# Last adds of a two-layer transformer stack written into the resident token rows, their transfers issued from two engines

## The chip, the cores and the metric

One core of a Trainium2 chip runs the whole kernel. The metric is the device time of one execution in microseconds (us). The kernel before was run five times: 1055.75, 1056.3, 1054.87, 1055.21 and 1051.39 us, with a median of 1055.21 us.

A core has five engines that run side by side, each with its own list of instructions: TensorE (PE, matmuls; its weight loads are shown apart as PEld), VectorE (DVE), ScalarE (ACT), GpSimd (POOL) and SyncE (SP). They wait for one another through semaphores. A transfer between the on-chip memory (SBUF) and the device memory (HBM) is issued by one of them, here mostly SP, and carried out by 16 DMA engines, which count a semaphore up, one step each, when their share has landed. Matmuls write into PSUM, a small memory of banks, from which DVE or ACT takes the results.

## The reference

The input is x, 2048 tokens of 256 numbers (f32). Four blocks are added to it one after the other, each reading the layer-normed tokens:

```python
x = x + _L0_xcond_ref(_layernorm(x), ctx, ctx, ...)    # 16-head attention over 1601 context rows
x = x + _L0_ffn_ref(_layernorm(x), ...)                # one of 8 experts for each token
x = x + _L1_xcond_ref(ctx, _layernorm(x), ...)         # attention in a window of the context
x = x + _L1_ffn_ref(_layernorm(x), ...)                # 64 slots
return x
```

The change lies in the end of the last one. There each token has weights `alpha` over 64 slots. The slots gather the tokens by these weights, go through a gated update and an attention among themselves, and give `slot_values`; then

```python
out = jnp.einsum('bts,bsd->btd', alpha, slot_values)
return out @ wo + bo
```

and the result is that plus x, 2048 x 256 numbers or 2 MB.

## The kernel before

The tokens live in SBUF from the first load to the end, in the tile `x_sb`, 128 partitions by 16 rows by 256 (token t*128 + p is row t of partition p). Every block adds its part to `x_sb` in place.

The first attention fills most of the span: for each block of 512 tokens and each group of four heads it searches the largest score of each token (L257, L262), computes scores and exponentials (L904, L909) and weighs the values (L870). Its order is written out by hand in Python as a list of steps that are put between the matmuls. Then come the experts (L1064, L1071), with the window attention and the slots' weights of earlier tokens as generators beside them: `aside` takes one step from each in turn. The program keeps the written order on each engine (`manual_schedule`), and the tile framework adds the semaphore waits. It knows which slice of a tile an instruction reads or writes.

The two generators leave behind, for each token block: `x_sb` with the window attention's part (L1258, POOL) and with the bias `bso` (L1335, POOL); the transposed weights `aT`, in which partitions 0 to 63 hold a rounded part and 64 to 127 the remainder (L1390, L1392); and the slots' sums in `psi`.

From L1439 on a single chain is left: the slots are updated, attend to one another, are normed (L1524) and are multiplied by the product of two weight matrices (L1527 to L1533). The result stands in PSUM as 128 x 256 and is split into two parts, by ACT (L1536) and DVE (L1537).

The last loop, L1541 to L1553, makes the output in eight turns of two token rows each (256 tokens). In each turn

- PE writes four matmuls into one PSUM bank (`f_ps`, L1546): for each of the two rows one with each part. `bank` hands out three banks in turn, so the matmuls of turn t wait until the add of turn t-3 has read its bank.
- DVE adds the bank to the rows of `x_sb`, one instruction of 128 x 512 (L1552), and writes the sum to a tile `o` of 2 KB in each partition. `o` comes from the pool `moe` with `bufs=3`, so there are three buffers, and the add of turn t waits until the transfer of turn t-3 has landed on all 16 DMA engines.
- SP issues the transfer of `o`, 256 KB, to the output (L1553), when the add is done.

Nothing else is left to do on ACT, POOL or the DMA engines in this loop. The program ends (L1629) when SP has seen the landing of all transfers, and the engines have met.

Of the kernel before, what the change touches and what calls it, by code (L numbers as in the profile page):

```python
# [10 lines left out]
F32 = mybir.dt.float32  # L11
# [4 lines left out]
ALU = mybir.AluOpType  # L16
# [3 lines left out]
P = 128  # L20
T = 2048
D = 256
# [40 lines left out]
def body(ctx: ExitStack, tc: tile.TileContext, a: dict, out: bass.AP):  # L63
    nc = tc.nc
# [5 lines left out]
    x_sb = keep.tile([P, NT, D], F32, name="x_sb")  # L70
# [109 lines left out]
    with (  # L180
# [49 lines left out]
        def two():  # L230
            return ps_s.tile([P, 2, LB], F32, tag="psc", name="s_ps")
# [508 lines left out]
        with (  # L740
# [137 lines left out]
            for u in range(NU):  # L878
                acc = None
                for i in range(NS):  # L880
# [16 lines left out]
                    for pl in range(2):  # L897
                        slot = (u * NS + i) * 2 + pl
                        look(slot)
                        ps = two()  # L900
# [35 lines left out]
    moe = ctx.enter_context(tc.tile_pool(name="moe", bufs=2))  # L936
# [7 lines left out]
    def bank(shape, name):  # L944
        n = int(np.prod(shape[1:]))
        ps = ps_pool.tile([P, LB], F32, tag="ps", name=name)[: shape[0], :n]
        if len(shape) == 3:
            ps = ps.rearrange("p (a b) -> p a b", a=shape[1])
        return ps
# [541 lines left out]
    for wt, b, name in ((wsq, bsq, "q4"), (wsk, bsk, "k4")):  # L1491
        ps = bank([NSLOT, NSLOT], name + "_ps")
# [10 lines left out]
    ps = bank([NSLOT, NSLOT], "qk_ps")  # L1503
# [11 lines left out]
    ps = bank([NSLOT, NSLOT], "pt_ps")  # L1515
# [3 lines left out]
    ps = bank([NSLOT, D], "sc_ps")  # L1519
# [8 lines left out]
    ps = bank([P, D], "s2_ps")  # L1528
# [11 lines left out]
    o_out = out.rearrange("(t p) d -> p t d", p=P)  # L1540
    for t2 in range(NT // 2):  # L1541
        ps = bank([P, 2, D], "f_ps")
        for k in range(2):
            t = t2 * 2 + k
            for w in range(2):
                nc.tensor.matmul(  # L1546
                    ps[:, k, :], aT[:, t * P : (t + 1) * P], parts[w],
                    start=w == 0, stop=w == 1,
                )
        o = moe.tile([P, 2, D], F32, name="o", bufs=3)  # L1550
        tl = slice(t2 * 2, t2 * 2 + 2)
        nc.vector.tensor_tensor(o, x_sb[:, tl, :], ps, ALU.add)  # L1552
        nc.sync.dma_start(o_out[:, tl, :], o)  # L1553


def lay_out(i):
# [76 lines left out]
```

## Time and profile before

| | us |
|---|---|
| median of the five runs | 1055.21 |
| the profiled execution | 1053.24 |
| its span | 1051.5 |
| span from the last split (L1536) to the end | 15.4 |
| DVE busy with the eight adds (L1552) | 5.2 |
| PE busy with the 32 matmuls of the loop (L1546) | 5.8 |
| idle time of DVE before an add, put down to transfers of `out_x` | 4.4 |

The span is the time from the first to the last instruction in the trace, and the profiled execution's own time is 1.7 us more. The profiled execution lies 2.0 us below the median. PE is busy for 90% of the whole span, DVE for 71%, ACT for 49%; in the last loop none of them is. A row of the page's groups gives an engine, a line, an operation, the tiles (output <- inputs), the shapes, the count, the busy time and the mean of one, and then how long the engine had been idle before, and for what. The chain of waits goes back from the last instruction, at each step to what released it.

### The profile page before, as it was taken

The page shows a single profiled execution, that of the slowest core. Times are in us where ns is not written, and L with a number is a line of the kernel's source. Part 1 is how long each engine was busy: PE and PEld are TensorE (multiplying, and loading weights), DVE is VectorE, ACT ScalarE, POOL GpSimd, SP SyncE. Part 2 cuts the span into 40 slices and gives each one's busy share as a digit, 9 for nine tenths or more (in the row PEclk, how much of TensorE's full clock was granted, in tenths as well). Part 3 has the DMA queues.
Part 4 walks back from the last instruction along what each step waited for, and adds up shares of the span by engine and source line. Part 5 has one row for each costly group of instructions (what it writes and reads, how often), then busy time and mean ns, then how long its engine had stood idle before and what let it go on. Part 6 is the DMA issues. An engine that isn't in the chain of part 4 may idle for free.

```text
span 1051.5 us, 14892 instructions
## 1 busy us (share of the span) xinstructions
PE 945.3 (90%) x5814; PEld 442.4 (42%) x5822; DVE 744.8 (71%) x1407; ACT 519.7 (49%) x614; POOL 71.8 (7%) x96
## 2 busy tenths in 40 slices
PE   7788888999988999998899999899979999989885
PEld 3244333444443344443343444343334464546543
DVE  7466868888877888877788887875054648585744
ACT  2423456676656666656666775667810012121430
POOL 4000200000010000000000000000030102111210
PEclk9998999999999999999999999989999999999998
DMA  5754721310102201101211011000080000000002
GB/s 173 162 148 101 145 74 46 110 29 2 29 2 82 65 2 29 29 1 39 82 29 29 2 29 29 1 2 1 2 230 1 1 0 1 1 1 0 1 1 81
DMA packets 32277, 46.98 MB, mean 45 GB/s; under 512 B 6411, under 2 KB 21268, under 8 KB 31950
## 3 DMA queue, kind: packets, MB, share of 16 engines
q1 hardware_dynamic: 30478, 43.65, 15.3%
q10 hardware_dynamic: 1232, 1.61, 0.4%
q8 instruction: 46, 0.75, 0.3%
q0 software_dynamic: 496, 0.76, 0.3%
q14 instruction: 25, 0.20, 0.1%
HBM read 26.77 MB, written 14.04 MB: 39 GB/s over the span
## 4 chain that ended last, share of the span: by engine, by line
PE 68%; DVE 25%; issue 4%; DMA 2%; ACT 1%; POOL 1%; POOLq 0%; SPq 0%; DVEq 0%; ACTq 0%
PE acc L870 18%; PE s_ps L904 14%; DVE mx L262 12%; PE a_ps L257 11%; PE y_ps L1064 7%; DVE xn L107 2%; DVE x_sb L1071 2%; PE a_ps L498 1%; PE o_ps L1250 1%; PE a_ps L845 1%; DVE ln_stats L96 1%; PE a_ps L240 1%; PE s_ps L627 1%; PE a_ps L284 1%; PE x_ps L461 1%
## 5 line engine op out<-in xcount | busy, mean ns | idle before, releaser
L262 DVE TENSOR_REDUCE mx<-a_ps 128x2 f32<-128x804 f32 (+1 forms) x637 | 490.8, 806 | 124.3 <-PE a_ps L257 117.7
L909 ACT ACTIVATE es<-s_ps 128x1024 f32<-128x1024 f32 (+1 forms) x416 | 408.3, 1022 | 201.9 <-PE s_ps L904 198.6
L257 PE MATMUL a_ps<-kb,qb 50*128 50x402 bf16 x992 | 218.1, 341 | 49.0 <-DVE mx L262 40.2
L904 PE MATMUL s_ps<-qt,kt 52*128 52x512 f32 (+1 forms) x832 | 236.7, 517 | 1.5 <-DMA qt<-nT 1.4
L870 PE MATMUL acc<-es,v 128*32 128x512 f32 (+1 forms) x1664 | 224.6, 611 | 0.0
L257 PEld LDWEIGHTS <-qb 50*128 50x128 bf16 x1024 | 77.5, 93 | 295.7 <-issue 281.9
L904 PE MATMUL s_ps<-ql,kt 52*128 52x512 f32 (+1 forms) x832 | 190.6, 394 | 0.0
L904 PEld LDWEIGHTS s_ps<-qt,kt 52*128 52x128 f32 (+1 forms) x832 | 97.1, 188 | 31.8 <-ACT es L909 16.7
L904 PEld LDWEIGHTS s_ps<-ql,kt 52*128 52x128 f32 (+1 forms) x832 | 103.0, 185 | 0.6
L1064 PE MATMUL y_ps<-expert_wT_sb,xT 128*128 128x512 f32 x192 | 89.8, 598 | 0.0
L102 POOL TENSOR_TENSOR ln_rstd<-ln_ve,mhalf 128x2 f32<-128x2 f32 (+2 forms) x28 | 21.1, 754 | 752.2 <-DVE ln_ve L100 750.9
L1071 DVE SCALAR_TENSOR_TENSOR x_sb<-y_ps,r_gate,x_sb 128x256 f32<-128x256 f32 x96 | 46.3, 482 | 32.5 <-PE y_ps L1064 30.7
L870 PEld LDWEIGHTS acc<-es,v 128*32 128x32 f32 (+1 forms) x1664 | 33.1, 108 | 42.3 <-issue 40.5
L1064 PEld LDWEIGHTS y_ps<-expert_wT_sb,xT 128*128 128x128 f32 x192 | 34.1, 191 | 31.9 <-issue 30.8
L1027 ACT COPY xT<-tr_ps 128x512 f32<-128x512 f32 (+1 forms) x28 | 13.4, 494 | 53.3 <-PE tr_ps L1024 53.3
L107 DVE TENSOR_SCALAR xn<-x_sb,ln_mv,ln_rstd 128x256 f32<-128x256 f32 x64 | 33.6, 568 | 1.1 <-POOL ln_rstd L102 1.1
L819 DVE RECIPROCAL rec<-a_ps 128x16 f32<-128x16 f32 x16 | 4.0, 253 | 42.7 <-PE a_ps L240 42.7
L1064 PE MATMUL y_ps<-expert_wT_sb,xnT 128*128 128x512 f32 x64 | 32.3, 632 | 0.0
L1024 PE MATMUL tr_ps<-ident,xn 128*128 128x128 f32 x88 | 17.6, 297 | 10.9 <-DVE xn L107 10.9
L96 DVE BATCH_NORM_STATS2 ln_stats<-x_sb 128x6 f32<-128x256 f32 x64 | 23.3, 413 | 3.4 <-POOL x_sb L1258 3.4
L1071 DVE SCALAR_TENSOR_TENSOR x_sb<-y_ps,gate,x_sb 128x256 f32<-128x256 f32 x32 | 15.5, 483 | 13.7 <-PE y_ps L1064 13.1
L997 PE MATMUL busy_ps<-xnT 128*128 128x512 bf16 x91 | 23.5, 387 | 0.4 <-issue 0.2
(347 smaller groups left out, 724.5 us busy)
## 6 DMA issues: line engine op xcount, KB each, us to landing
qt<-q_rows SPq DMA_DIRECT2D x32, 192.0 KB
q_rows<-qhi SPq DMA_DIRECT2D x8, 512.0 KB
qb<-q_rows SPq DMA_DIRECT2D x30, 96.0 KB
kt<-expert_wT_sb SPq DMA_DIRECT2D x24, 100.5 KB
q_rows<-qp SPq DMA_DIRECT2D x8, 256.0 KB
q_rows<-qlo SPq DMA_DIRECT2D x8, 256.0 KB
ql<-q_rows SPq DMA_DIRECT2D x32, 64.0 KB
expert_wT_sb<-in_expert_wT SPq DMA_DIRECT2D x1, 2048.0 KB
```

The lines of the kernel that those rows point to most:

```text
L96: nc.vector.bn_stats(stats[:rows, i, :], src[:, i, :])
L102: nc.gpsimd.tensor_tensor(rstd[:rows, :n], ve[:rows, :n], mhalf[:rows, :n], ALU.pow)
L107: nc.vector.tensor_scalar(dst[:, i, :], src[:, i, :], mv[:rows, i, 0:1], rstd[:rows, i : i + 1], ALU.subtract, ALU.mult,)
L257: nc.tensor.matmul(ps[:, k, :CH], qb[u % 2][rows, pl, t * P : (t + 1) * P], kb[g][rows, pl, c * CH : (c + 1) * CH], start=True, stop=True,)
L262: nc.vector.tensor_reduce(flat[:, n : self.n], ps[:, : self.n - n, :CH], AX.X, ALU.max)
L870: nc.tensor.matmul(acc[HP * j : HP * (j + 1), :], v[:n, i, h * VW : h * VW + HP], es[j // 2][:n, j % 2, :], start=i == 0, stop=i == NS - 1,)
L904: nc.tensor.matmul(ps[:n, h, :], kt[u % NG][rows, pl, i * P : i * P + n], q[u % nq][rows, pl, :], start=k == 0, stop=k == 1,)
L909: nc.scalar.activation(e[:n], ps[:n], AF.Exp)
L997: nc.tensor.matmul(calm[0].rearrange("p e d -> p (e d)"), xnT[:, 1, :P].bitcast(BF16)[:, 1::2], xnT[:, 0, :].bitcast(BF16)[:, 1::2], start ...
L1024: nc.tensor.transpose(ps[:, t * P : (t + 1) * P], xn[:, t, c * P : (c + 1) * P], ident)
L1064: nc.tensor.matmul(ps.rearrange("p e d -> p (e d)"), xT[:, c, tok], ew[:, c, pair * 2 * D : (pair + 1) * 2 * D], start=c == 0, stop=c == 1,)
L1071: nc.vector.scalar_tensor_tensor(xb[:, t, :], ps[:, k, :], gate[:, t, e : e + 1], xb[:, t, :], ALU.mult, ALU.add,)
```

## The change

The tile `o` is gone. The add writes its sum over the two token rows that it has read, in `x_sb`, and the transfer reads from there. The transfers of the even turns are issued by SP, as before, those of the odd turns by ACT.

```diff
-        o = moe.tile([P, 2, D], F32, name="o", bufs=3)
         tl = slice(t2 * 2, t2 * 2 + 2)
-        nc.vector.tensor_tensor(o, x_sb[:, tl, :], ps, ALU.add)
-        nc.sync.dma_start(o_out[:, tl, :], o)
+        nc.vector.tensor_tensor(x_sb[:, tl, :], x_sb[:, tl, :], ps, ALU.add)
+        (nc.scalar if t2 % 2 else nc.sync).dma_start(o_out[:, tl, :], x_sb[:, tl, :])
```

In the list of instructions with their waits, nothing else differs. The eight adds wait for PE alone, where five of the eight waited for a transfer as well. SP issues four transfers in place of eight, and ACT four after its last copy (L1536). The lines after the loop have moved up by one, so that the add is L1551, the transfer L1552 and the end of the program L1628.

## Prediction

> **What bounds the kernel now.** I read the end first, since the list of instructions differs only in the last loop. The busy time by stage gives the frame: from 1036 to 1051.5 us PE is busy 5.9 us of 15.5, DVE 5.6, ACT 0.4. No engine bounds this stage. The chain of waits, asked for its last part (start, duration, what), shows what does:
>
> ```profile
> 1037.66 0.70 DVE o L1552
> 1038.36 0.02 issue
> 1038.37 4.40 DMA out_x<-o
> ...
> 1042.89 0.70 DVE o L1552
> 1043.59 0.02 issue
> 1043.61 2.17 DMA out_x<-o
> ...
> 1045.90 0.70 DVE o L1552
> ...
> 1046.68 0.69 DVE o L1552
> ```
>
> Two landings, 4.40 and 2.17 us, stand between adds: the three buffers of `o` are full, and the fourth add waits for the first transfer, the seventh for the fourth. The views of the waits, first DVE's, then SP's (waiting line <- what for: total, times, longest), say the same and add the end of the program:
>
> ```profile
> DVE o L1552 <- DMA out_x<-o: 4.4, 2, 3.4
> ```
>
> ```profile
> SPq L1629 <- DMA out_x<-o: 2.3, 2, 1.7
> ```
>
> One landing takes 4.40 us and the other 2.17 for the same 256 KB. The view of the transfer's line gives the least, median and greatest time of one issue in ns, and the table of 1-us windows gives the engines' busy time, the granted clock, and last the DMA engines' mean share and rate:
>
> ```profile
> L1553 SPq DMA_DIRECT2D out_x<-o x8: 372/373/2092, 1038.4 to 1047.4; - x8
> ```
>
> ```profile
> 1040.00:1041.00 1.00, 0.34 (x3) 0.13 (x2) 0.00 (x0) 0.00 (x0) 0.00 (x0) 1.00 0.77 263
> 1041.00:1042.00 1.00, 0.00 (x0) 0.00 (x0) 0.00 (x0) 0.00 (x0) 0.00 (x0) 1.00 0.05 10
> 1042.00:1043.00 1.00, 0.00 (x0) 0.00 (x0) 0.11 (x1) 0.00 (x0) 0.00 (x0) 0.52 0.80 268
> ```
>
> From 1041 to 1042 the 16 DMA engines are nearly idle although a third transfer has been asked for. The trace's packet records say why. At 1039.53 one 16 KB packet of instructions (queue q8) starts and takes 1.74 us. The page counts 46 such packets, one for about every 128 PE instructions, so I take them for PE's code. It occupies one DMA engine: of the 16 steps of the first transfer's semaphore 15 come by 1040.56, the last at 1042.77; of the second, by 1041.28 and at 1043.41; of the third, by 1043.41 and at 1044.04. SP's third issue, begun at 1039.57, ends only at 1041.66, 0.39 us after that packet. Other issues begun during such a packet behave alike: at 317.34 (1.68 us long) and 484.92 (1.14 us) they end 0.37 and 0.39 us after theirs. So a code packet here holds up one DMA engine by 2.2 us and any new issue until 0.4 us after its end.
>
> **The change part by part.** All is counted on the profiled execution: span 1051.46, time 1053.24, last landing 1050.18, and 1.28 us from there to the end of the span.
>
> *Taken away: the wait for a buffer.* The first three adds, which no transfer holds, start at 1037.66, 1038.26 and 1038.86, so 0.60 apart. Eight at that pace: the last starts at 1037.66 + 7 x 0.60 = 1041.86 and ends at 1042.55, not 1047.37. PE keeps up, as four matmuls take 0.58 of these 0.60 us, and its bank comes free with the add three turns before. DVE's end is thus 4.8 us earlier. But the end is set by landings, and what is late next is the transfers.
>
> *Writing in place.* Nothing reads these rows of `x_sb` later but their transfer. L1084 is the same add over its own input, 128 x 512 with PSUM beside it; the view of the line gives least, median and greatest ns:
>
> ```profile
> L1084 DVE TENSOR_TENSOR x_sb<-x_sb,eb_ps x8: 680/688/689, 800.4 to 981.3; 128x512 f32<-128x512 f32 x8
> ```
>
> L1552 has 680/686/690. The price is 0.
>
> *The transfers.* Each gives every DMA engine 16 KB. Where three follow one another without a gap (the fourth to the sixth), they land at 1045.78, 1046.55 and 1047.28: 0.75 apart. The adds come every 0.60, so from the first transfer on the DMA engines have a backlog, and the order or the issuing engine no longer matters. Two ends:
>
> - The held DMA engine. Up to 1040 nothing differs, since PE reaches the same instruction at the same time (the adds that it waits for until then are the first three, which wait for no transfer). So the packet comes at 1039.53 again, and this engine lands its first share at 1042.77. Seven more follow. Alone it needs 0.64 for each (1042.77, 1043.41, 1044.04), beside the others 0.75: last landing 1042.77 + 7 x 0.64 = 1047.2 to 1042.77 + 7 x 0.75 = 1048.0.
> - The 15 others. If the third and fourth issues are again held until 1041.66, they land the third transfer at 1043.41 and five more at 0.75: 1047.2.
>
> I take the middle of the first, 1047.6, as it is the later: 1050.18 - 1047.6 = **2.6 us earlier** (2.2 to 3.0).
>
> *The second queue.* SP and ACT issue in 0.37 to 0.53 us (ACT: five rows at the start of the trace, 0.39 to 0.53). With one queue the last five issues would end at 1041.66 + 5 x 0.42 = 1043.8 (0.42: 0.37 and the wait instruction and gap after it), while the sixth transfer is still being moved; so dividing them is worth 0 here. Nothing is queued behind the waiting ACT instructions but the end of the program. Behind SP's, its waits for the landings: eight, as before, about 0.06 each.
>
> *The trace's other packet.* An 8 KB code packet (q14) at 1047.99 makes one engine's last step of the last transfer 0.66 late (1050.18 against 1049.52). Its predecessors come every 128 to 134 DVE records, so I take it for DVE's; DVE now has five waiting instructions fewer and reaches that place after the last landing or never. Its going is part of the 2.6 us, and if it hits the held engine instead, 0.66 are given back.
>
> The sum: 1053.24 - 2.6 = 1050.6 for an execution like the profiled one. That one lay 2.0 us under the median of the runs, so against the median I predict 1055.21 - 2.6 = **1052.6**.
>
> **The rivals.**
>
> *B, the code packet doesn't hold the end.* Then the transfers run through: first landing 1040.56 + 7 x 0.75 = 1045.8, 4.4 us earlier, 1050.8. For it: the packet took 1.74 us here and mostly 0.9 to 1.3 elsewhere, so the hold may be smaller with other neighbours, and a second queue could let the other engines go on. Against it: all three landings above show the hold. Between 3.2 and 4.4: 1050.8 to 1052.0. Chance 0.25. The Trainium skill, Runtime: NRT & Kernel Launch, section Instruction fetch mechanics, says that crossing into a new block of code costs one tail-bump of a DMA and is mostly hidden; by that rule this rival would hold. The trace agrees that PE itself doesn't wait, but not for the transfers.
>
> *C, less than forecast.* The held engine now serves three queues, SP's, ACT's and the code's. If the code packet grows by as much again as it has over its usual time (1.74 - 1.0 = 0.7 us) and the 8 KB packet falls on the same engine (0.66), the gain is 2.6 - 1.4 = 1.2: 1054.0. For it: the packet was longest here, where the queues were full. Against it: the engine's work is the same number of bytes. From 1053.2 to 1055.0: chance 0.2.
>
> *D, slower: ACT's issues are dear.* The odd transfers are in series on ACT. The last lands at 1038.97 + 4c + 1.8 us, where c is the time of one issue and 1.8 lies between the end of the first issue (1038.76) and its 15 landings (1040.56). The time is worse than before from c = 2.35 on. The dearest issue in the trace took 2.83 us (SP, at 775.83, among the 2 MB of weight loads): then 1052.1, 1.9 us later, 1057.1; from c = 3.15 on it is over 0.3%. Against it: ACT's five issues at the start, also back to back among loads, took 0.53 at most. Chance 0.04.
>
> That the change doesn't do what it says (that the adds wait for transfers of other rows of `x_sb`) is excluded by the list of instructions: they wait for PE alone; chance 0.01, counted with D. If each add waited for the landing before it, the loop would take eight times some 2.9 us.
>
> **How the numbers follow.** The forecast (2.2 to 3.0 us gained, 1052.2 to 1053.0) has 0.50, B 0.25, C 0.20, D 0.05. About 0.3%, or 3.2 us, is what a measurement of this kernel can tell from no change, and its five runs lie 4.9 us apart. B is faster by that; so is a quarter of the forecast with the scatter of the medians: 0.25 + 0.13 = 0.38. D is half slower by that, with some of the scatter 0.04. The rest, 0.58, is within it. The range takes in B's and C's ends, and 1 us below and 0.4 above for the scatter of a median: 1049.8 to 1055.4.
>
> **What would show it.** In the changed profile: the adds (L1551) follow each other at 0.60 us from 1037.7 to 1042.5, and no DVE time is put down to `out_x`; queue q10 has 1 MB more and q1 1 MB less; one 16 KB packet near 1039.5; the issues begun in it are long, the others 0.4; the DMA share from 1042.2 on is 0.9 or more without a gap, and one engine's last step comes last, near 1047.6. The prediction is wrong if the packet moves (B), if the last landing lags the adds by more than 6 us (C), or if an ACT issue takes over 2 us without that packet (D).

## The result, and the profile after

The changed kernel takes 1052.01 us (median of 38 runs), the kernel before 1055.19 us (64 runs): a ratio of 0.9968, with a 95% interval of 0.9960 to 0.9977. That is 3.4 us less by the ratio, where 2.6 was forecast, and just past the bound of 0.3%; the forecast gave the greater chance to the near side of that bound. The interval allows 2.4 to 4.2 us, so the time alone doesn't rule out 2.6. The profiled execution takes 1051.8 us, with a span of 1050.0.

The last pieces of the chain of waits of the changed kernel (start, duration, what) hold no transfer between adds any more:

```profile
1038.91 0.63 PE f_ps L1546 x3
1039.54 0.02 issue
1039.57 4.28 DVE x_sb L1551 x7
1043.84 0.60 DVEq L1628
```

The chain as printed ends with DVE's last instruction. The wait behind it stands in the waits of SP's queue (waiting line <- what for: total, times, longest):

```profile
SPq L1628 <- DMA out_x<-x_sb: 4.4, 2, 3.8
```

Before, this was 2.3 us: DVE is done sooner, and the program's end waits longer for the transfers. The view of the add's line (least, median, greatest ns; first and last start) and that of the issues:

```profile
L1551 DVE TENSOR_TENSOR x_sb<-x_sb,f_ps x8: 680/681/690, 1039.6 to 1043.8; 128x512 f32<-128x512 f32 x8
```

```profile
L1552 SPq DMA_DIRECT2D out_x<-x_sb x4: 373/378/384, 1040.3 to 1043.9; - x4
L1552 ACTq DMA_DIRECT2D out_x<-x_sb x4: 378/426/961, 1040.9 to 1044.5; - x4
```

Eight adds in 4.87 us with none waiting for a transfer, SP's issues all short, one of ACT's of 0.96 us. The windows of 1 us (last two columns: DMA share and GB/s) show the transfers without the hole that the kernel before had from 1041 to 1042:

```profile
1041.00:1042.00 1.00, 1.00 (x9) 0.94 (x8) 1.00 (x3) 0.00 (x0) 0.00 (x0) 1.00 0.82 261
1042.00:1043.00 1.00, 1.00 (x9) 0.87 (x8) 1.00 (x3) 0.00 (x0) 0.00 (x0) 1.00 0.98 328
1043.00:1044.00 1.00, 0.44 (x4) 0.23 (x2) 1.00 (x3) 0.00 (x0) 0.00 (x0) 1.00 1.00 321
...
1046.00:1047.00 1.00, 0.00 (x0) 0.00 (x0) 0.00 (x0) 0.00 (x0) 0.00 (x0) 1.00 1.02 345
1047.00:1048.00 1.00, 0.00 (x0) 0.00 (x0) 0.00 (x0) 0.00 (x0) 0.00 (x0) 0.57 0.48 169
1048.00:1049.00 1.00, 0.00 (x0) 0.00 (x0) 0.00 (x0) 0.00 (x0) 0.00 (x0) 0.50 0.03 9
```

The last row shows the end of what one DMA engine still does alone: the last of the 16 steps of the last landing comes at 9.19 us after the first add, the step before it at 8.34, 0.85 us earlier.

Spans compare badly here. The first add starts at 1037.66 in the profile of before and at 1039.57 in that of the changed kernel, though the program up to there is the same; over all twelve profiles of this study it starts between 1037.43 and 1042.13. The profiled execution of before was a quick one, 2.0 us under the median, that of the changed kernel only 0.2. So everything below is counted from the start of the first add to the last landing: 12.52 us before, **9.19** after. The 3.33 us between them agree with the 3.4 of the ratio (the two medians are 3.2 apart).

### The profile page after: what moved, and what is told of

Its sections match the earlier page's. It is cut to its first block, busy times and chain, and to the rows that moved or that the text cites. A ratio compares the mean times of both kernels' runs of the same rounds, so it can differ in the third digit from the quotient of the medians.

```text
span 1050.0 us, 14887 instructions
## 1 busy us (share of the span) xinstructions
PE 944.2 (90%) x5814; PEld 441.1 (42%) x5822; DVE 744.7 (71%) x1407; ACT 519.4 (49%) x614; POOL 71.8 (7%) x96
## 4 chain that ended last, share of the span: by engine, by line
PE 67%; DVE 25%; issue 4%; DMA 1%; POOL 1%; ACT 1%; SPq 0%; POOLq 0%; DVEq 0%; ACTq 0%
PE acc L870 18%; PE s_ps L904 14%; DVE mx L262 12%; PE a_ps L257 11%; PE y_ps L1064 7%; DVE xn L107 2%; DVE x_sb L1071 2%; PE a_ps L498 2%; DVE ln_stats L96 1%; PE o_ps L1250 1%; PE a_ps L845 1%; PE a_ps L240 1%; PE s_ps L627 1%; PE a_ps L284 1%; PE x_ps L461 1%
```

## The experiments

My theory after the result: the gain is that no add waits for a buffer; that wait was dear because the landing waited for was the one held up by PE's last code packet; and what is left is that packet and the DMA engines' time for 2 MB. The rivals: the second queue brings the gain; one DMA engine is slow for another reason; writing in place has a price of its own.

The table is from the trace's records of transfers and semaphores, in us from the start of the first add. "Held step" is the last of the 16 steps of the first landing, "15 others" the step before it. The ratio is to the kernel before in the same session and is not the quotient of two medians of this table: the kernel before had 1054.49 us beside e1 to e4 and 1055.15 beside e5 to e8.

| kernel | code packet: start, length | 15 others | held step | last landing | median | ratio (95%) |
|---|---|---|---|---|---|---|
| before | 1.87, 1.74 | 2.90 | 5.11 | 12.52 | 1055.19 | 1 |
| changed | 1.83, 1.36 | 2.93 | 4.54 | 9.19 | 1052.01 | 0.9968 (0.9960 to 0.9977) |
| e1: in place, SP alone | 1.92, 1.46 | 2.92 | 4.88 | 9.53 | 1051.92 | 0.9983 (0.9969 to 0.9996) |
| e2: `o`, two queues | 1.76, 1.56 | 2.90 | 4.81 | 12.16 | 1054.53 | 1.0001 (0.9984 to 1.0018) |
| e3: changed, no packet | none | 2.90 | 2.93 | 8.27 | 1050.32 | 0.9972 (0.9956 to 0.9988) |
| e4: before, no packet | none | 2.85 | 2.88 | 10.22 | 1052.27 | 0.9989 (0.9977 to 1.0000) |
| e5: other rows, SP alone | 1.75, 1.30 | 3.00 | 4.55 | 9.21 | 1052.33 | 0.9975 (0.9954 to 0.9997) |
| e6: e1, no packet | none | 2.90 | 2.94 | 8.29 | 1052.61 | 0.9969 (0.9950 to 0.9987) |
| e7: changed, 2 KB rows | 1.83, 1.56 | 2.83 | 4.88 | 9.26 | 1051.40 | 0.9971 (0.9954 to 0.9988) |
| e8: e7, no packet | none | 2.85 | 2.85 | 7.60 | 1050.96 | 0.9959 (0.9944 to 0.9975) |
| e9: before again | 1.71, 1.77 | 2.88 | 4.99 | 12.27 | 1053.44 (one run) | - |
| e10: changed again | 1.85, 1.34 | 2.93 | 4.51 | 9.16 | 1051.69 (one run) | - |

The times move by tenths of a per cent with intervals as wide, since the whole span scatters. The verdicts rest on the last landings, each from one profiled execution. The two kernels that were profiled twice give last landings 0.25 us apart (before and e9) and 0.03 us apart (changed and e10), so differences of 0.2 us between two rows are not shown by them alone.

### e1: in place, one queue

```diff
-        (nc.scalar if t2 % 2 else nc.sync).dma_start(o_out[:, tl, :], x_sb[:, tl, :])
+        nc.sync.dma_start(o_out[:, tl, :], x_sb[:, tl, :])
```

> Sums in place, but all eight transfers issued by SP. Measured mainly from the start of the first add to the last landing: before 12.52 us (1037.66 to 1050.18), changed kernel 9.18 us (1039.57 to 1048.75). Theory (the gain is the wait for a buffer, the second queue is worth nothing): 8.9 to 9.5 us, a time within 0.1% of the changed kernel. Rival (with one queue the third issue is held through the code packet, as before, and the other 15 DMA engines run dry): third transfer lands on 15 engines 5.75 us after the first add, five more at 0.75 make 9.5, the held engine up to 10.3: 0.4 to 1.1 us later than the changed kernel.

9.53 us, just past the theory's range and short of the rival's, so nearly all of the gain (2.99 of 3.33 us) is there with one queue. The times can't add to this: the medians are alike (1051.92 and 1052.01 us), the ratios differ by 0.15%, within their intervals. The rival's mechanism is seen too, in the view of SP's issues (least, median, greatest ns): one, the third, takes 1.83 us and ends 0.40 us after the code packet.

```profile
L1552 SPq DMA_DIRECT2D out_x<-x_sb x8: 384/438/1833, 1040.2 to 1045.6; - x8
```

The 0.34 us that it ends later than the changed kernel are taken apart below, with e6.

### e2: three buffers, two queues

```diff
-        nc.sync.dma_start(o_out[:, tl, :], o)
+        (nc.scalar if t2 % 2 else nc.sync).dma_start(o_out[:, tl, :], o)
```

> The three buffers of o as before, only the odd transfers issued by ACT. Theory: the fourth add still waits for the last step of the first landing (4.5 to 5.1 us after the first add) and the seventh for the fourth landing, so 11.5 to 12.5 us from the first add to the last landing, 0 to 1 us less than before. Rival (the queue is what matters): near 9.2 us as in the changed kernel.

12.16 us, as the theory says. The adds still wait, as DVE's waits show, for 4.1 us where before had 4.4:

```profile
DVE o L1552 <- DMA out_x<-o: 4.1, 2, 3.1
```

No issue is held here. SP's second, the third of all, begins 0.15 us after the start of the code packet and takes 0.38 us; the fourth comes when the packet is over:

```profile
L1553 SPq DMA_DIRECT2D out_x<-o x4: 372/378/384, 1038.3 to 1046.2; - x4
L1553 ACTq DMA_DIRECT2D out_x<-o x4: 378/385/408, 1038.9 to 1047.0; - x4
```

### e3: the changed kernel without the code packet

```diff
-        for _ in range(n if calm else 0):
+        for _ in range(n - (n > 1) if calm else 0):
```

> The changed kernel with one matmul fewer in each call of busy that issues two or more (23 matmuls whose result nobody reads are left out), so that PE's last 16 KB code packet, some 16 PE instructions ahead of the end, is not reached. Theory (the code packet holds one DMA engine and with it the end): no q8 packet in the last loop, all 16 engines land together, 2.93 + 7 x 0.75 = 8.2 us from the first add, some 0.9 us less than the changed kernel. Rival (the lagging step of each landing has another cause, such as a slower DMA engine): one step still comes about 0.9 to 1.6 us late, 9.2 us.

8.27 us, and in each landing the last of the 16 steps comes within 0.03 us of the step before it. The rest of the loop is as it was: the adds 0.60 us apart, 15 steps of the first landing at 2.90 us against 2.93. The view of the DMA queues over the last loop, first of e3, then of the changed kernel (packets, MB, share of 16 engines), differs by the one packet on q8:

```profile
q1 hardware_dynamic: 1088, 1.05, 32.1%
q10 hardware_dynamic: 1088, 1.05, 31.1%
```

```profile
q1 hardware_dynamic: 1088, 1.05, 31.9%
q10 hardware_dynamic: 1088, 1.05, 30.8%
q8 instruction: 1, 0.02, 0.8%
```

One 16 KB packet costs the changed kernel 0.9 us. ACT's issues are short with it gone:

```profile
L1552 ACTq DMA_DIRECT2D out_x<-x_sb x4: 378/384/404, 1038.7 to 1042.3; - x4
```

### e4: the kernel before without the code packet

The same edit of `busy` in the kernel before.

> The kernel before with the same 23 matmuls left out. Theory (the wait for a buffer costs so much because the landing that it waits for is the held one): the fourth add starts at 2.95 us after the first instead of 5.24, and the last landing comes at 9.6 to 10.2 us instead of 12.52, so that the buffers alone cost 1.3 to 2 us against e3 and not 3.3. Rival (the buffers cost the same with or without the packet): 11.5 us or more.

10.22 us, just past the range, and the fourth add starts at 3.01. DVE's wait for transfers falls from 4.4 to 1.9 us:

```profile
DVE o L1552 <- DMA out_x<-o: 1.9, 2, 1.1
```

So the packet cost the kernel before 2.3 us and costs the changed one 0.9. The buffers cost 1.95 us without the packet (10.22 against 8.27) and 3.33 with it. In the kernel before the hold was paid in the wait for a buffer, so that it delayed the last five adds and not one DMA engine alone.

### e5: not in place, but without a wait

```diff
-        o = moe.tile([P, 2, D], F32, name="o", bufs=3)
         tl = slice(t2 * 2, t2 * 2 + 2)
+        o = xn4[:, tl, 0:D]
```

> The sums are not written in place but into a tile of 16 rows that nobody reads any more (xn4), all transfers from SP. Theory (the gain is that no add waits for a buffer; writing in place is only one way to get there): the adds 0.60 us apart as in e1, 9.53 us from the first add to the last landing, 9.4 to 9.7. Rival (reading and writing the same rows is itself cheaper or dearer): adds of other than 0.68 us, or an end off by more than 0.3 us.

9.21 us, a little below the range that I gave; the adds are 0.60 us apart and take 0.68 us, as in place:

```profile
L1552 DVE TENSOR_TENSOR xn<-x_sb,f_ps x8: 680/682/690, 1039.4 to 1043.6; 128x512 f32<-128x512 f32 x8
```

Where the sum is written doesn't matter, as long as no one waits for the place. The miss of 0.2 us goes with the code packet, which ends 0.33 us earlier here than in e1 (3.05 against 3.38); the last landing is 0.32 us earlier.

### e6: in place, one queue, no code packet

The edits of e1 and e3 together.

> Sums in place, all transfers from SP, and the 23 matmuls of e3 left out, so no code packet. Theory (the second queue's 0.34 us, e1 9.53 against 9.19, come from the third issue that the code packet holds): all issues of SP take about 0.38 us and the last landing comes at 8.27 us, as in e3. Rival (the second queue is worth something by itself, by shorter issues or two streams on each DMA engine): 8.5 us or more.

8.29 us against 8.27: without the packet the second queue is worth nothing that shows. Not as expected were SP's last three issues: 0.56, 0.66 and 0.66 us instead of 0.38, with three or four transfers outstanding (the fourth and fifth, with three, took 0.37). The DMA engines had work meanwhile, so it cost nothing.

```profile
L1552 SPq DMA_DIRECT2D out_x<-x_sb x8: 372/384/661, 1042.9 to 1047.2; - x8
```

With the packet, the last landing comes 4.65 us after the held step in the changed kernel, e1 and e10, and 4.66 in e5. So the 0.34 us between e1 and the changed kernel lie ahead of the held step: 0.19 are a packet that ended later (3.38 against 3.19), and 0.15 a held step that comes 1.50 us after the packet's end and not 1.35. Whether the second queue has a part in these 0.15 is not shown. The step comes 1.33 us after the packet's end in e10, but 1.50 and 1.49 in e2 and e7, which issue from two queues as well, and e5, with one queue, ends at 9.21 us, as early as the changed kernel.

### e7 and e8: fewer, larger packets

```diff
-            x_in = a["x"].rearrange("(t p) d -> p t d", p=P)
+            x_in = a["x"].rearrange("(p t) d -> p t d", p=P)
-    o_out = out.rearrange("(t p) d -> p t d", p=P)
+    o_out = out.rearrange("(p t) d -> p t d", p=P)
```

e8 has the edit of e3 as well.

> The changed kernel with tokens laid out so that each partition holds 16 neighbouring tokens (x and the output are both read and written as 128 x 16 rows of 256): a turn's 2 KB of each partition are contiguous in the output, so each DMA engine moves 8 packets of 2 KB instead of 16 of 1 KB. In the trace of before packets of 1 KB take 46 ns and of 2 KB 84 ns. Theory (the tail is the DMA engines' time for packets): 0.68 us for each transfer instead of 0.75, so 8.5 to 8.8 us from the first add to the last landing. Rival (bytes and the HBM's rate set the pace): 9.2 us as in the changed kernel.

> e7 with the 23 matmuls of e3 left out as well. Theory: 2.85 + 7 x 0.68 = 7.6 us from the first add to the last landing, the shortest end of all, a ratio to the kernel before of about 0.995. Rival (rate): 8.3 us as in e3.

e7 missed: 9.26 us, no gain. The 15 others did land at the pace of 2 KB packets as long as they had work (2.83, 3.50, 4.14), but ACT's second issue, held until 0.39 us after the code packet, took 1.27 us, SP's third, begun 0.25 us before the packet's end, 0.65 us, and the held engine set the end. Without the packet the theory holds to the digit: 7.60 us, the shortest end, and the best ratio of all. Over its eight us the queues carry the same bytes in 1152 packets instead of 2176:

```profile
DMA packets 1152, 2.10 MB, mean 262 GB/s; under 512 B 128, under 2 KB 128, under 8 KB 1152
```

### e9 and e10: both kernels once more

> The kernel before, unchanged, for a second profile. The prediction took 1.74 us for the code packet and 5.11 us for the held step of the first landing (after the first add). Theory (the packet's length varies from execution to execution, 1.30 to 1.74 us in the six profiles that hold it, and 1.74 was a long one; the held step comes 1.5 us after its end): a packet of 1.3 to 1.6 us, the held step at 4.5 to 4.9 us, the last landing at 11.9 to 12.3 us. Rival (before's pattern of transfers makes it long): 1.7 us or more again, the last landing at 12.5 us.

> The changed kernel, unchanged, for a second profile. Theory: the last landing comes 4.65 us after the held step of the first, as in the changed kernel, e1 and e5 (4.65, 4.65, 4.66), and that step 1.35 to 1.5 us after the end of the code packet; with a packet of 1.3 to 1.74 us the end is at 9.1 to 9.8 us. Rival (the end doesn't follow the packet): 9.2 us whatever its length.

The kernel before has a packet of 1.77 us, after 1.74, and the held step at 4.99; both are outside the theory's ranges, and the packet is as the rival has it, while the last landing, 12.27, is inside. The changed kernel has a packet of 1.34 us, after 1.36, and ends at 9.16, again 4.65 us behind the held step, as the theory says.

I had taken the packet's length for a matter of chance. Two pairs that agree within 0.03 us, with 0.4 us between the two kernels, speak for a length that belongs to the program (the others have 1.30 to 1.56). Two profiles of each don't prove it: the fourth code packet from the end took 1.12 us in the first profile of before and 1.39 in the second. The second pair of profiles puts the gain at 3.11 us, the first at 3.33.

## Why the prediction was right, and where its size was off

- *The place.* Right. The last landing is 3.33 us earlier against the first add, about the whole gain of the ratio, so nothing that shows is left over for the rest of the program.
- *The wait for a buffer goes, and the transfers are late next.* Right: the last add starts 4.19 us after the first (forecast 4.20), and the end is set by the held engine, not by DVE. e1 and e5 show that the missing wait is the gain: they have it with one queue, e5 without writing in place, and e2, with the wait and two queues, doesn't.
- *Writing in place costs nothing.* Right: 681 ns against 686, and e5 is the same without it.
- *The held engine sets the end.* Right in mechanism, mis-sized in the term: the held step was taken over from the profile of before, at 5.11 us, on the ground that nothing differs until then. It came at 4.54: 0.42 us earlier because the packet ended at 3.19 and not at 3.61 (it took 1.36 us and not 1.74), and 0.15 because the step followed the packet's end by 1.35 us and not 1.50. The seven transfers after it took 4.65 us, between the 4.5 and 5.2 of the forecast, but 0.2 under the middle. 0.57 and 0.2 are the 0.75 us by which the forecast's end (1047.6, or 9.94 after the first add) was late, and what carried the result over 0.3%. The gain of 3.33 us is thus outside the forecast's own 2.2 to 3.0 and inside B's 3.2 to 4.4; the number alone would have spoken for B, and only the late step in the trace tells them apart.
- *The issues in the packet.* Half right. The third issue, SP's second, began in the packet and took 0.38 us; the fourth, ACT's second, was held until 0.28 us after it. In e2 none is held. With one queue it is the third (before, e9, e1, e5). That a code packet holds any new issue was read from too few rows: in the same trace of before, issues begun during a code packet at 224.77, 393.00 and 524.33 us took 0.56, 0.65 and 0.56 us and ended before the packet. As the third issue wasn't held, the 15 other DMA engines were done 8.34 us after the first add and not at the 9.5 (1047.2) of the forecast.
- *The second queue is worth 0.* Right without the packet (e6 against e3). With it at most some 0.15 us, and whether it is the queue's is open (see e6). The price of an issue was too low: with one queue the last five took 0.42 to 0.66 us each in e1, not 0.37, and it cost nothing. The Trainium skill, DMA: Bandwidth & Descriptors, section Issuing engines are not separate DMA queues, says that transfers from several engines run on the same 16 DMA engines and that only issue time is saved. e6 agrees, 8.29 against 8.27.
- *The 8 KB packet leaves the loop.* Right: it comes 11.64 us after the first add, after the last landing. In before and in e4 it makes the last two landings 0.6 to 0.8 us late.
- *B, the packet doesn't hold the end.* Wrong, and priced by e3: without it the end is 0.92 us earlier still. The rule of the Trainium skill (Runtime: NRT & Kernel Launch, Instruction fetch mechanics), that such a fetch is mostly hidden, holds for PE, which is busy 1.00 of each of the windows from 1041 to 1043 of the changed kernel, where the packet falls, but not for a transfer beside it: e3 and e4 put it at 0.9 and 2.3 us. *C and D* did not occur; the longest ACT issue of the changed kernel was 0.96 us.

Open stays why the code packet takes 1.74 and 1.77 us in one program and 1.30 to 1.56 in others, and which outstanding transfers let an issue be held: the third on one queue, the fourth on two, none in e2. Neither was tried apart.

## What to carry to other kernels

A loop that ends a program with one add and one store for each turn can run into the wait for a buffer: three buffers for eight turns cost 3.3 us here. Rows that the add reads and nobody needs later are places for its results at no cost. Eight places were enough; how many between three and eight would do was not tried. A second queue beside the three buffers took away at most 0.4 us (e2). When a store's landing seems long, look for the one step of its semaphore that is late, and for a code packet on the instruction queues at that moment. Here it cost more where an engine waited for that landing, 2.3 us against 0.9. Where a change gains a fraction of a per cent, count from an event close to it: the span here scatters by more than the gain.

## What the runs showed of the hardware

- A 16 KB packet of PE's code of 1.30 to 1.77 us, in a stream of stores, held one of 16 DMA engines until 1.3 to 1.5 us after its end, while the others landed their shares of the transfers that had been issued (15 steps of the first landing at 2.8 to 3.0 us, the last at 4.5 to 5.1).
- These packets come with the count of PE's instructions, in the last stretch one for every 112 to 151 weight loads and about as many matmuls. With 23 matmuls fewer (5791 in the trace of e3 against 5814) there are 45 of them and not 46, and none falls into the loop.
- With all eight stores on one queue, SP's last issues, begun with three or four transfers outstanding, took 0.56 to 0.66 us (e6) instead of 0.38; others with three outstanding took 0.37.
- Transfers of 256 KB to HBM that follow one another land every 0.76 us at packets of 1 KB and every 0.68 at 2 KB (e3 and e8: 5.34 and 4.75 us for seven).
